# One-hots of two batches in one instruction, sums of sixteen tiles, and 48 columns of each column tile by VectorE, in a graph-attention kernel

## The chip, the core and the metric

The kernel runs on one core of a Trainium2 chip. The core has five engines with a queue each: TensorE (PE in the profile; its weight loads are listed apart as PEld), VectorE (DVE), ScalarE (ACT), GpSimd (POOL) and SyncE (SP), and 16 DMA engines that all of them share. An engine's sequencer takes the instructions of its queue in order; register loads, semaphore waits and the issuing of DMAs are done by the sequencer itself (DVEq, ACTq, SPq, POOLq in the profile) and do not count as busy time of the engine.

The metric is the device time of one execution in microseconds. It is measured over several runs, and the median is taken. Besides, one execution is recorded by the hardware profiler; its span runs from the first to the last instruction.

## What is computed

One layer of graph attention over 6250 nodes and 206250 edges, sorted by their destination `dst`, with 8 heads of 16 features. Cut to what matters, the reference is:

```
Qh = (x @ WQ).reshape(N, 8, 16);  Kh, Vh likewise with WK, WV
Eh = (edge_attr @ WE).reshape(E, 8, 16)
score = einsum('ehd,ehd,ehd->eh', Kh[src], Qh[dst], Eh) / sqrt(16)
score = exp(clip(score, -5, 5))
wV = segment_sum(Vh[src] * score[:, :, None], dst, N)
Z  = segment_sum(score, dst, N)
out = layernorm(x + (wV / (Z[:, :, None] + 1e-6)).reshape(N, 128))
```

## The kernel before

**Tiles and batches.** The edges are cut into 1612 tiles of 128. A batch (`cut_batches`) is four tiles; the last eight tiles make three batches of two and two of one, so there are 406 batches. In the head of the program a table `kv` of K and V rows of all nodes is made from `x` and written to HBM. Then one loop over the batches runs, written out in full. From batch 12 (`XB`) on, the order of the instructions on every engine is the order in which the program issues them (`tc.manual_schedule`); before that a planner of the framework orders them.

**One iteration b of the loop**, in the order in which it issues:

- Loads on SP: edge features (`load_chunk`, tiles of eight edge tiles in the pool `edges` with five buffers, two chunks ahead), the destination numbers relative to a window (`load_rel`), and Q rows (`load_q`).
- `stage_a(b)`, TensorE: `eps` (edge features times WE, L453) into the one PSUM buffer of `psE`, and `qps` (L456), which expands the Q rows to the edges by a one-hot `onehotT`.
- `gather` (L401), GpSimd: one indirect DMA for each edge tile fetches the 128 rows of `kv` into `kvrows`, twelve batches of buffers. A gather for batch b waits until TensorE has expanded batch b - `lag(b)`; the lag falls from 12 to 3 in the course of the run.
- `finish`, whenever two blocks of 128 nodes are complete: TensorE adds up the window sums that reach into the two blocks, each moved to its place by a shift matrix (`add_windows`, L492, into `finps`), ScalarE copies the result (`fin`), and a layernorm is put on a list. Its steps, some 22 small VectorE instructions beginning with `rz` (L727), are issued one at a time at the four `fill()` places of later iterations. The five steps that make 128 Q rows (`q_rows`, on VectorE `qst` and `qr`) go to the same places.
- VectorE, in this order: `kq` of batch b-1 (L463), one-hot of batch b+2 (`stage_0`, L431), fill, `kqe` of b-1 (L466), `onehotT` of b+2 (`stage_0t`, L441), fill, the reduce to `sc` of b-1 (L469), `msg` of b-2 (L507), column copies (L371), fill, the clip of `sc` (L472), fill. So in a batch each instruction of the chain kq, kqe, reduce has a one-hot of another batch between it and its successor.
- ScalarE: column copies (L374) in two portions, `place_columns` (L390), and `weigh` of b-1, which makes the weights that `msg` will need (L479, L480).
- `stage_c` of b-2, TensorE: the one-hot sums the messages of each tile into `agg` (L529). `project_columns`: a matmul makes K and V rows from a finished column tile (`colkv`, L383).

**Column tiles.** For 163 batches the fourth tile is not gathered. Its 128 columns of `x` are copied one by one from the transposed `x` in SBUF, to `xcol`, and projected by TensorE. The addresses are loaded into registers of the engine that copies, a run at a time: on ScalarE eleven runs of eight columns, one copy each; on VectorE five runs of eight columns, where one instruction takes two columns. `columns` issues as many runs as a due formula asks for up to this batch; `COLP`, `COLA` and `COLV` set the rate and the runs:

```
due = int((b - COL0 + COLL - 1 + share) * runs * COLP[1] / COLP[0] + 1e-6)
```

**One-hots and sums.** Eight consecutive tiles have their destinations inside a window of nodes. The first four tiles use a half of 64 nodes at its beginning, the other four one that begins 16 nodes later (`HALF`), and the two sets of buffers `halves` hold the one-hots of either kind, with the unused 64 columns set to zero once. `agg` holds two windows side by side; after 16 tiles ScalarE copies both to `sum` (L539).

**Edge numbers.** In the head, `from_window` reads the destinations of the edges (`dB_sb`), subtracts the first of each window (`relq`, L192) and stores them to HBM (`relD`, L193), from where `load_rel` reads them back. 128 rows come in the head, the other 74 at batch 14.

Of the kernel before, what the change touches and what calls it, by code (L numbers as in the profile page):

```python
# [20 lines left out]
B = 4  # L21
G = 4
HW = 64
HALF = 16
DRIFT = 24
MW = D + H
CH = 8
# [2 lines left out]
LOCK = XB + 6  # L30
STEP = 3
GLEAD = 2
OHB = (3, 5)
TAIL = 8
LAST = NT - TAIL
QL = N // P
# [11 lines left out]
QLOOK = 3  # L48
QREG = 16
COL0 = 24  # L50
COLP = (7, 3)
COLA = (8, 11)
COLV = (8, 5)
COLL = 8
RING = 4096
SUMS = 8
XT_AT = RING + P
NB = (N + P - 1) // P

# [16 lines left out]
    return [B * min(COL0 + k * COLP[0] // COLP[1], last - (n - 1 - k)) + B - 1 for k in range(n)]  # L76


def pair_of(t):

    return (t // (2 * G), t // G % 2) if t < LAST else (NT, 1)


def pair_start(k):

    return (2 * k * G * N + NT // 2) // NT - DRIFT


def window_start(t):
    k, half = pair_of(t)  # L90
    return QL * P + HW if k == NT else pair_start(k) + HALF * half


def q_built(j):
# [5 lines left out]
def edge_attention(ctx: ExitStack, tc: tile.TileContext, x, xT, srcT, srcC, dstT, dstB, dst0, bnd, lo, eaT,  # L100
# [24 lines left out]
    iota_f = cp.tile([P, P], F32, name="iota_f")  # L125
    shift = cp.tile([P, 3 * P], F32, name="shift")
    ident = cp.tile([P, P], F32, name="ident")
    halves = [[cp.tile([P, B, P], F32, name=f"onehot{h}{i}") for i in range(OHB[h])] for h in range(2)]
    cnt_i = cp.tile([1, 1], I32, name="cnt_i")

    batches = cut_batches()
# [8 lines left out]
    with ExitStack() as fast:  # L140
# [8 lines left out]
        nc.vector.tensor_scalar(shift[:HW], io_i[:HW], 0, None, op0=ALU.is_equal)  # L149
        nc.vector.tensor_scalar(shift[HW:], io_i[HW:], HALF - HW, None, op0=ALU.is_equal)  # L150
# [31 lines left out]
        def from_window(i):  # L182

            a, k = i * P, min(P, NJ - i * P)
            if i == len(dB_sb):
                dB_sb.append(ip.tile([P, WT * P], I32, name="dB_sb", bufs=1))
                nc.sync.dma_start(dB_sb[i][:k], dstB[a:a + k])
            d = dB_sb[i]
            w = ip.tile([P, 1], F32, name="wq0", bufs=2)
            nc.vector.tensor_tensor(w[:k], d[:k, :1], bnd_c[:k, i:i + 1], op=ALU.min)  # L190
            r = ip.tile([P, WT * P], BF16, name="relq", bufs=1)
            nc.vector.tensor_scalar(r[:k], d[:k], w[:k], None, op0=ALU.subtract)  # L192
            nc.sync.dma_start(relD[a:a + k], r[:k])  # L193
            cl = wp.tile([P, WT * P], F32, name="clq", tag="kvst", bufs=2)
            count(k, cl[:k], r[:k], QW - 1)
# [132 lines left out]
        def load_chunk(c):  # L328
            if c in chunks or c * CH >= NT:
                return  # L330
            n = min(CH, NT - c * CH) * P
            tl = ep.tile([P, CH * P], F32, name="ea")
            nc.sync.dma_start(tl[:, :n], eaT[:, c * CH * P:c * CH * P + n])
            chunks[c] = tl

# [8 lines left out]
            return max(STEP, 12 - (b - LOCK) // 40)  # L344

        col_tiles, xT_bytes = {}, spread.bitcast(U8)
        used = [0, 0]

        copied, projected = {}, []

        def columns(eng, b, share=1.0):

            size, runs = COLA if eng is nc.scalar else COLV
            first = 0 if eng is nc.scalar else COLA[0] * COLA[1]
            engine = mybir.EngineType.Activation if eng is nc.scalar else mybir.EngineType.DVE
            copy = eng.copy if eng is nc.scalar else eng.tensor_copy
            due = int((b - COL0 + COLL - 1 + share) * runs * COLP[1] / COLP[0] + 1e-6)
            while copied.get(engine, 0) < min(due, len(col_batches) * runs):
                k, j = divmod(copied.get(engine, 0), runs)
# [4 lines left out]
                at = nc.values_load_multi_w_load_instructions(  # L364
                    col_at[k % col_half:k % col_half + 1, k // col_half, j:j + size], engines=(engine,),
                    min_val=XT_AT, max_val=XT_AT + 8 * (N - 1) + 4,
                    skip_runtime_bounds_check_because="edges name nodes")[1]
                if eng is nc.vector:
                    for c in range(0, size, 2):
                        both = [xT_bytes[:, ds(a - XT_AT, 8)] for a in at[c:c + 2]]  # L370
                        eng.tensor_tensor(to[:, 4 * (j + c):4 * (j + c) + 8], *both, op=ALU.bitwise_or)  # L371
                    continue
                for c in range(size):
                    copy(to[:, 4 * (j + c):4 * (j + c) + 4], xT_bytes[:, ds(at[c] - XT_AT, 4)])  # L374
# [37 lines left out]
        def project(g, n):  # L412
# [6 lines left out]
            for i in range(0, n, 2):  # L419
# [3 lines left out]
                    nc.tensor.matmul(pk[:, j, :], xgT[:, i + j, :], wkv_sb, start=True, stop=True)  # L423
                nc.scalar.copy(g[:, i:i + k, :], pk[:, :k, :])

        def stage_0(b):
            t0, n = batches[b][0], len(batches[b])
            half = pair_of(t0)[1]
            oh = halves[half][used[half] % OHB[half]]
            used[half] += 1  # L430
            nc.vector.tensor_tensor(oh[:, :n, HW * half:HW * half + HW],  # L431
                                    iota_p[:, None, :].to_broadcast([P, n, HW]),
                                    rel[:, t0:t0 + n, None].to_broadcast([P, n, HW]), op=ALU.is_equal)
            st8[b] = oh, None

        def stage_0t(b):
            t0, n = batches[b][0], len(batches[b])
            oh = st8[b][0]
            ohT = wp.tile([QROWS, B * P], BF16, name="onehotT", bufs=AHEAD + 2)
            e0 = t0 % RC * P  # L440
            nc.vector.tensor_scalar(ohT[:, :n * P], rels[t0 // RC][:, e0:e0 + n * P], node[:QROWS], None,  # L441
                                    op0=ALU.is_equal)
            st8[b] = oh, ohT

        def stage_a(b, g):
            t0, n = batches[b][0], len(batches[b])
# [35 lines left out]

        def windows(q):

            return [(k, pair_start(k) - q * P) for k in range(min(NT, LAST + 2 * G - 1) // (2 * G))
                    if -HW - HALF < pair_start(k) - q * P < P]

        def add_windows(ps, q, first, stop):

            parts = windows(q)  # L490
            for i, (k, s) in enumerate(parts):
                nc.tensor.matmul(ps, shift[:, P - s:2 * P - s], sums[k // 2][:, k % 2],  # L492
                                 start=first and i == 0, stop=stop and i == len(parts) - 1)

        def finish(j):
# [16 lines left out]
        def stage_c(b):  # L512
            n, g, oh, m = st8.pop(b)
            for i in range(n):
                t = batches[b][i]
                k, half = pair_of(t)
# [5 lines left out]
                u = k if final else k // 2  # L522
                first = u not in aggs
                if first:
                    aggs[u] = psA.tile([P, 2, MW], F32, name="agg")
                    if final:
                        add_windows(aggs[u][:, 0], QL, True, False)
                tail = k == NT if t == NT - 1 else pair_of(t + 1)[0] != k
                nc.tensor.matmul(aggs[u][:, 0 if final else k % 2], oh[:, i, :], m[:, i, :],  # L529
                                 start=not final and t % (2 * G) == 0, stop=tail)  # L530
                if tail and final:
                    norms.extend(pending)
                    pending.clear()
                    while norms:
                        fill()
                    norms.append(layernorm(nc, sp, aggs.pop(u)[:, :1], xbs.pop(QL), out, QL, 1, stores))
                elif tail and (k % 2 == 1 or t == LAST - 1):
                    sums[u] = sp.tile([P, 2, MW], F32, name="sum", bufs=SUMS)
                    nc.scalar.copy(sums[u][:, :k % 2 + 1], aggs.pop(u)[:, :k % 2 + 1])  # L539
                    while len(finished) < QL // 2 and all(v // 2 <= u for v, _ in windows(2 * len(finished) + 1)):  # L540
                        ready.append(len(finished))
                        finished.append(u)

        gathered = {b: gather(b) for b in range(2)}
        for b0 in range(0, NB, KB):
# [251 lines left out]
```

## Time and profile before

| | us |
|---|---|
| median of 3 runs (lowest, highest) | 1867.37 (1865.28, 1867.83) |
| the profiled execution | 1864.63 |
| its span | 1862.8 |
| PE busy | 1331.3 |
| DVE busy | 1679.4 |
| ACT busy | 1623.1 |
| POOL busy | 1379.9 |

Rows of the profile are read as follows. A group: line, engine, operation, what it writes and reads, shapes, count, then busy time and the mean duration in ns, then the idle time just before the group's instructions and what ended most of it. A row of the waits: who waited for whom, the total in us, how often, the longest. A row of the timeline: start, duration, engine, line, operation; in square brackets idle time before it and its releaser, where "issue" is time in which the engine waited for nothing that the profile shows. A row of a table by stages: the stretch, its length, the busy time of the engine asked for with the number of instructions (x), the granted TensorE clock, the DMA share and GB/s. A row of one line: engine, operation, count, shortest, median and longest duration in ns, and the start of the first and the last in us. The mean granted TensorE clock of the profiled execution is 0.919.

### The profile page before, as it was taken

The numbers are of one execution on the slowest core, as the hardware profiler recorded it, in microseconds if no ns is written. First come the engines' busy times: TensorE is split into PE (matmuls) and PEld (weight loads), VectorE is DVE, ScalarE is ACT, GpSimd is POOL, SyncE is SP. The second block draws the span as 40 slices with busy tenths as digits, with TensorE's granted clock in tenths as the row PEclk, the third lists the DMA queues.
The fourth block names the chain that finished last, engine by engine and source line by source line (L and its number), as shares of the span: only waits on it lengthen the run. The fifth ranks groups of instructions, "written<-read, shape, count | busy, mean of one in ns | idle before, by whom it ended". The sixth has DMA issues, their size and how long they took to land.

```text
span 1862.8 us, 48831 instructions
## 1 busy us (share of the span) xinstructions
PE 1331.3 (71%) x9376; PEld 1163.7 (62%) x9376; DVE 1679.4 (90%) x6911; ACT 1623.1 (87%) x15506; POOL 1379.9 (74%) x1456
## 2 busy tenths in 40 slices
PE   4787777677776777676777776777767767677676
PEld 3576666666675666565666665666656656666665
DVE  3479999999999999999999999998999899998997
ACT  1236999899999999999999999999899999998993
POOL 6577777777777777777777777777777777777774
PEclk8898999899989998999999999898899899888998
DMA  9767757767777587677667667667766676667662
GB/s 316 220 196 213 219 179 209 207 201 207 207 215 208 180 241 199 184 217 228 192 209 228 190 191 225 203 185 214 219 203 186 195 231 191 195 192 227 207 195 70
DMA packets 171087, 381.63 MB, mean 205 GB/s; under 512 B 58478, under 2 KB 84412, under 8 KB 170774
## 3 DMA queue, kind: packets, MB, share of 16 engines
q0 software_dynamic: 68768, 186.80, 34.2%
q1 hardware_dynamic: 100866, 190.58, 33.7%
q14 instruction: 237, 1.94, 0.3%
q8 instruction: 76, 1.25, 0.3%
q10 hardware_dynamic: 1140, 1.06, 0.2%
HBM read 363.50 MB, written 14.81 MB: 203 GB/s over the span
## 4 chain that ended last, share of the span: by engine, by line
DVE 49%; PE 15%; DMA 12%; issue 6%; DVEq 6%; POOL 3%; ACT 0%; POOLq 0%
DMA kvrows<-kv,src 12%; DVE kqe L466 9%; DVE kq L463 9%; DVE xcol L371 8%; PE eps L453 6%; DVE sc L469 6%; DVE msg L507 5%; DVEq L364 5%; DVE onehot L431 5%; DVE onehotT L441 4%; PE agg L529 4%; POOL kvrows L401 3%; PE finps L492 3%; DVE sc L472 2%; PE qps L456 1%
## 5 line engine op out<-in xcount | busy, mean ns | idle before, releaser
L401 POOL DMA_INDIRECT kvrows<-kv,src x1401 | 1333.3, 952 | 441.9 <-issue 315.5
L374 ACT COPY xcol<-xT_sb 128x4 uint8 x14344 | 1442.7, 191 | 39.9 <-issue 33.9
L453 PE MATMUL eps<-we_sb,ea 128*128 128x128 f32 x3224 | 493.0, 300 | 446.5 <-issue 224.1
L453 PEld LDWEIGHTS eps<-we_sb,ea 128*128 128x128 f32 x3224 | 429.9, 206 | 538.6 <-issue 449.1
L529 PE MATMUL agg<-msg,onehot 128*128 128x136 f32 x3224 | 536.3, 314 | 34.0 <-DVE msg L507 23.2
L529 PEld LDWEIGHTS agg<-msg,onehot 128*128 128x128 f32 x3224 | 457.0, 212 | 86.1 <-DVE msg L507 83.5
L371 DVE TENSOR_TENSOR xcol<-xT_sb 128x8 uint8 x3260 | 301.8, 160 | 24.8 <-issue 22.2
L463 DVE TENSOR_TENSOR kq<-kvrows,qps 128x512 f32<-128x512 f32 x406 | 274.5, 676 | 51.0 <-DMA kvrows<-kv,src 26.7
L507 DVE TENSOR_TENSOR msg<-kvrows,exp_p 128x512 f32<-128x512 f32 x406 | 272.1, 670 | 4.0 <-ACT exp_p L480 4.0
L466 DVE TENSOR_TENSOR kqe<-kq,eps 128x512 f32<-128x512 f32 x406 | 272.9, 672 | 1.2 <-PE eps L453 0.8
L469 DVE TENSOR_REDUCE sc<-kqe 128x32 f32<-128x512 f32 x406 | 271.1, 668 | 0.2
L456 PE MATMUL qps<-qw,onehotT 126*128 126x128 bf16 x1612 | 169.6, 230 | 0.4 <-DVE kq L463 0.4
L431 DVE TENSOR_TENSOR onehot<-iota_p,dst_sb 128x256 f32<-128x256 f32 x406 | 167.4, 413 | 0.4 <-PE agg L529 0.4
L441 DVE TENSOR_SCALAR onehotT<-relb,node 126x512 bf16<-126x512 bf16 x406 | 148.3, 366 | 5.3 <-PE qps L456 2.7
L479 ACT ACTIVATE msg<-sc 128x32 f32<-128x32 f32 x406 | 92.9, 229 | 65.5 <-DVE sc L472 61.6
L456 PEld LDWEIGHTS <-onehotT 126*128 126x128 bf16 x1612 | 135.2, 104 | 9.4 <-issue 0.6
L383 PE MATMUL colkv<-wkv_sb,xcol 128*128 128x256 f32 x326 | 108.7, 418 | 0.0
L472 DVE TENSOR_SCALAR sc<-sc 128x32 f32<-128x32 f32 x406 | 84.5, 208 | 0.4
L492 PE MATMUL finps<-sum,shift 128*128 128x136 f32 x640 | 80.0, 282 | 0.0
L492 PEld LDWEIGHTS finps<-sum,shift 128*128 128x128 f32 x640 | 76.5, 191 | 0.0
L480 ACT ACTIVATE exp_p<-sc 128x32 f32<-128x32 f32 x406 | 74.1, 183 | 0.0
L401 POOL DMA_INDIRECT kvrows<-x,src x48 | 45.7, 952 | 21.2 <-issue 11.9
(73 smaller groups left out, 553.4 us busy)
## 6 DMA issues: line engine op xcount, KB each, us to landing
ea<-eaT SPq DMA_DIRECT2D x201, 512.0 KB
relb<-relD SPq DMA_DIRECT2D x100, 504.0 KB
kvrows<-kv,src POOLq DMA_INDIRECT x1401
qw<-qs SPq DMA_DIRECT2D x202, 31.5 KB
kv<-kvst SPq DMA_DIRECT2D x12, 512.0 KB
xT_sb<-xT SPq DMA_DIRECT2D x10, 521.0 KB
qs<-qst SPq DMA_DIRECT2D x48, 96.0 KB
xb<-x SPq DMA_DIRECT2D x24, 128.0 KB
```

The lines of the kernel that those rows point to most:

```text
L371: eng.tensor_tensor(to[:, 4 * (j + c):4 * (j + c) + 8], *both, op=ALU.bitwise_or)
L374: copy(to[:, 4 * (j + c):4 * (j + c) + 4], xT_bytes[:, ds(at[c] - XT_AT, 4)])
L401: ins = nc.gpsimd.indirect_dma_start(out=g[:k, i, :f], out_offset=None, in_=rows, in_offset=bass.IndirectOffsetOnAxis(ap=src_col(t)[:k], a ...
L431: nc.vector.tensor_tensor(oh[:, :n, HW * half:HW * half + HW], iota_p[:, None, :].to_broadcast([P, n, HW]), rel[:, t0:t0 + n, None].to_bro ...
L441: nc.vector.tensor_scalar(ohT[:, :n * P], rels[t0 // RC][:, e0:e0 + n * P], node[:QROWS], None, op0=ALU.is_equal)
L453: nc.tensor.matmul(pe[:, i, :], ea[:, i * P:i * P + P], we_sb, start=True, stop=True)
L456: expanded[b] = nc.tensor.matmul(pq[:, i, :], ohT[:, i * P:i * P + P], loaded[t0 // WT], start=True, stop=True)
L463: nc.vector.tensor_tensor(t0[:, :n], g[:, :n, :D], pq[:, :n], op=ALU.mult)
L466: nc.vector.tensor_tensor(t1[:, :n], t0[:, :n], pe[:, :n], op=ALU.mult)
L469: nc.vector.tensor_reduce(sc[:, :n], t1[:, :n].rearrange("p b (h d) -> p b h d", h=H), axis=AX.X, op=ALU.add)
L507: nc.vector.tensor_tensor(m[:, :n, :D].rearrange("p b (h d) -> p b h d", h=H), g[:, :n, D:].rearrange("p b (h d) -> p b h d", h=H), exp_p[ ...
L529: nc.tensor.matmul(aggs[u][:, 0 if final else k % 2], oh[:, i, :], m[:, i, :], start=not final and t % (2 * G) == 0, stop=tail)
```

## The change

The one-hots of two neighbouring batches are made by one instruction each (`onehot` and `onehotT`), where both batches have four tiles; the second of the two batches then issues none. The buffers are five tiles for two batches. A one-hot block keeps its 64 columns at a fixed place, with zeros around it, and a tile's offset in its window (0, 16, 32 or 48) is made by reading the block from so many columns earlier. Thus 16 tiles share one window of 128 nodes with one sum (`agg` and `sum` hold one window, not two), and `windows` lists fewer sums for each block of nodes. There are 167 column tiles, seven in 16 batches where there were three in seven; ScalarE copies ten runs of eight columns of each, VectorE six. The edge numbers go to a buffer of the pool `edges` and are loaded where `from_window` is called.

```diff
-HALF = 16
+QUAD = 4
+STEPS = 16
-OHB = (3, 5)
+OHB = 5
-COLP = (7, 3)
-COLA = (8, 11)
-COLV = (8, 5)
+COLP = (16, 7)
+COLA = (8, 10)
+COLV = (8, 6)
-SUMS = 8
+SUMS = 9
...
+def window_of(t):
+
+    return (t // (QUAD * G), STEPS * (t // G % QUAD)) if t < LAST else (NT, HW)
...
+def first_node(k):
+
+    return (QUAD * k * G * N + NT // 2) // NT - DRIFT
...
-    halves = [[cp.tile([P, B, P], F32, name=f"onehot{h}{i}") for i in range(OHB[h])] for h in range(2)]
+    onehots = [cp.tile([P, HW + 2 * B * P], F32, name=f"onehot{i}") for i in range(OHB)]
...
-        for h in range(2):
-            for tl in halves[h]:
-                nc.vector.memset(tl[:, :, HW - HW * h:P - HW * h], 0.0)
+        for tl in onehots:
+            nc.vector.memset(tl[:, :HW], 0.0)
+            nc.vector.memset(tl[:, HW:].rearrange("p (t n) -> p t n", n=P)[:, :, HW:], 0.0)
         nc.vector.tensor_copy(iota_f, io2)
-        dB_sb = [ip.tile([P, WT * P], I32, name="dB_sb", bufs=1)]
-        nc.scalar.dma_start(dB_sb[0][:min(P, NJ)], dstB[:min(P, NJ)])
...
-            if i == len(dB_sb):
-                dB_sb.append(ip.tile([P, WT * P], I32, name="dB_sb", bufs=1))
-                nc.sync.dma_start(dB_sb[i][:k], dstB[a:a + k])
-            d = dB_sb[i]
+            d = ep.tile([P, WT * P], I32, name="dB_sb", tag="ea")
+            (nc.sync if i else nc.scalar).dma_start(d[:k], dstB[a:a + k])
...
-                    col_tiles[k] = wp.tile([P, P], F32, name="xcol", bufs=4)
+                    col_tiles[k] = wp.tile([P, P], F32, name="xcol", bufs=5)
...
+        def together(b):
+
+            t0 = batches[b][0]
+            n = len(batches[b])
+            if n == B and b + 1 < nbat and len(batches[b + 1]) == B and t0 % (2 * B) == 0:
+                return [b, b + 1]
+            return [] if n == B and t0 % (2 * B) else [b]
+
         def stage_0(b):
...
+            group = together(b)
+            if not group:
+                return
+            t0, n = batches[b][0], sum(len(batches[i]) for i in group)
+            tl = onehots[used[0] % OHB]
+            used[0] += 1
+            nc.vector.tensor_tensor(tl[:, HW:].rearrange("p (t n) -> p t n", n=P)[:, :n, :HW],
                                     iota_p[:, None, :].to_broadcast([P, n, HW]),
                                     rel[:, t0:t0 + n, None].to_broadcast([P, n, HW]), op=ALU.is_equal)
-            st8[b] = oh, None
+            for i in group:
+                st8[i] = tl, HW + (batches[i][0] - t0) * P - window_of(batches[i][0])[1], None
 
         def stage_0t(b):
...
-            ohT = wp.tile([QROWS, B * P], BF16, name="onehotT", bufs=AHEAD + 2)
+            ohT = wp.tile([QROWS, 2 * B * P], BF16, name="onehotT", bufs=3)
...
-            return [(k, pair_start(k) - q * P) for k in range(min(NT, LAST + 2 * G - 1) // (2 * G))
-                    if -HW - HALF < pair_start(k) - q * P < P]
+            return [(k, first_node(k) - q * P) for k in range((LAST - 1) // (QUAD * G) + 1)
+                    if -HW - STEPS * (QUAD - 1) < first_node(k) - q * P < P]
...
-                nc.tensor.matmul(aggs[u][:, 0 if final else k % 2], oh[:, i, :], m[:, i, :],
-                                 start=not final and t % (2 * G) == 0, stop=tail)
+                nc.tensor.matmul(aggs[k][:, 0], oh[0][:, oh[1] + i * P:oh[1] + i * P + P], m[:, i, :],
+                                 start=not final and t % (QUAD * G) == 0, stop=tail)
...
-                elif tail and (k % 2 == 1 or t == LAST - 1):
-                    sums[u] = sp.tile([P, 2, MW], F32, name="sum", bufs=SUMS)
-                    nc.scalar.copy(sums[u][:, :k % 2 + 1], aggs.pop(u)[:, :k % 2 + 1])
+                elif tail:
+                    sums[k] = sp.tile([P, MW], F32, name="sum", bufs=SUMS)
+                    nc.scalar.copy(sums[k], aggs.pop(k)[:, 0])
```

More of the change, by code (lines that the diff above doesn't have):

```diff
@@ L76, in column_tiles @@
     return [B * min(COL0 + k * COLP[0] // COLP[1], last - (n - 1 - k)) + B - 1 for k in range(n)]
[L79 to L86, printed above, removed]
+def window_of(t):
+    return (t // (QUAD * G), STEPS * (t // G % QUAD)) if t < LAST else (NT, HW)
+def first_node(k):
+    return (QUAD * k * G * N + NT // 2) // NT - DRIFT
 def window_start(t):
-    k, half = pair_of(t)
-    return QL * P + HW if k == NT else pair_start(k) + HALF * half
+    k, at = window_of(t)
+    return (QL * P if k == NT else first_node(k)) + at
 def q_built(j):
@@ L331, in load_chunk @@
             n = min(CH, NT - c * CH) * P
-            tl = ep.tile([P, CH * P], F32, name="ea")
+            tl = ep.tile([P, CH * P], F32, name="ea", tag="ea")
             nc.sync.dma_start(tl[:, :n], eaT[:, c * CH * P:c * CH * P + n])
@@ L346, in edge_attention @@
         col_tiles, xT_bytes = {}, spread.bitcast(U8)
-        used = [0, 0]
+        used = [0]
         copied, projected = {}, []
@@ L424, in project @@
                 nc.scalar.copy(g[:, i:i + k, :], pk[:, :k, :])
-        def stage_0(b):
[L427 to L431, printed above, removed]
+        def together(b):
[4 more added lines that the diff above has]
+            return [] if n == B and t0 % (2 * B) else [b]
+        def stage_0(b):
+            group = together(b)
[5 more added lines that the diff above has]
+            nc.vector.tensor_tensor(tl[:, HW:].rearrange("p (t n) -> p t n", n=P)[:, :n, :HW],
                                     iota_p[:, None, :].to_broadcast([P, n, HW]),
                                     rel[:, t0:t0 + n, None].to_broadcast([P, n, HW]), op=ALU.is_equal)
-            st8[b] = oh, None
+            for i in group:
+                st8[i] = tl, HW + (batches[i][0] - t0) * P - window_of(batches[i][0])[1], None
         def stage_0t(b):
-            t0, n = batches[b][0], len(batches[b])
-            oh = st8[b][0]
-            ohT = wp.tile([QROWS, B * P], BF16, name="onehotT", bufs=AHEAD + 2)
+            group = together(b)
+            if not group:
+                return
+            t0, n = batches[b][0], sum(len(batches[i]) for i in group)
+            ohT = wp.tile([QROWS, 2 * B * P], BF16, name="onehotT", bufs=3)
             e0 = t0 % RC * P
@@ L442, in stage_0t @@
                                     op0=ALU.is_equal)
-            st8[b] = oh, ohT
+            for i in group:
+                tl, at, _ = st8[i]
+                k = (batches[i][0] - t0) * P
+                st8[i] = (tl, at), ohT[:, k:k + len(batches[i]) * P]
         def stage_a(b, g):
@@ L491, in add_windows @@
             for i, (k, s) in enumerate(parts):
-                nc.tensor.matmul(ps, shift[:, P - s:2 * P - s], sums[k // 2][:, k % 2],
+                nc.tensor.matmul(ps, shift[:, P - s:2 * P - s], sums[k],
                                  start=first and i == 0, stop=stop and i == len(parts) - 1)
@@ L515, in stage_c @@
                 t = batches[b][i]
-                k, half = pair_of(t)
+                k, _ = window_of(t)
                 q = t * N // NT // P
@@ L521, in stage_c @@
                 final = k == NT
[L522 to L525, printed above, removed]
+                if k not in aggs:
+                    aggs[k] = psA.tile([P, 1, MW], F32, name="agg")
                     if final:
-                        add_windows(aggs[u][:, 0], QL, True, False)
-                tail = k == NT if t == NT - 1 else pair_of(t + 1)[0] != k
-                nc.tensor.matmul(aggs[u][:, 0 if final else k % 2], oh[:, i, :], m[:, i, :],
-                                 start=not final and t % (2 * G) == 0, stop=tail)
+                        add_windows(aggs[k][:, 0], QL, True, False)
+                tail = t == NT - 1 or window_of(t + 1)[0] != k
+                nc.tensor.matmul(aggs[k][:, 0], oh[0][:, oh[1] + i * P:oh[1] + i * P + P], m[:, i, :],
+                                 start=not final and t % (QUAD * G) == 0, stop=tail)
                 if tail and final:
@@ L535, in stage_c @@
                         fill()
-                    norms.append(layernorm(nc, sp, aggs.pop(u)[:, :1], xbs.pop(QL), out, QL, 1, stores))
-                elif tail and (k % 2 == 1 or t == LAST - 1):
-                    sums[u] = sp.tile([P, 2, MW], F32, name="sum", bufs=SUMS)
-                    nc.scalar.copy(sums[u][:, :k % 2 + 1], aggs.pop(u)[:, :k % 2 + 1])
-                    while len(finished) < QL // 2 and all(v // 2 <= u for v, _ in windows(2 * len(finished) + 1)):
+                    norms.append(layernorm(nc, sp, aggs.pop(k), xbs.pop(QL), out, QL, 1, stores))
+                elif tail:
+                    sums[k] = sp.tile([P, MW], F32, name="sum", bufs=SUMS)
+                    nc.scalar.copy(sums[k], aggs.pop(k)[:, 0])
+                    while len(finished) < QL // 2 and all(v <= k for v, _ in windows(2 * len(finished) + 1)):
                         ready.append(len(finished))
-                        finished.append(u)
+                        finished.append(k)
         gathered = {b: gather(b) for b in range(2)}
```

3 lines of the change are left out of this document (1 added, 2 removed).

## The prediction

> **What bounds the kernel now.** I read the page's busy times first, then the gather line, then two tables of the same eight stages (GpSimd's gathers, VectorE's kq), then VectorE's waits, and last VectorE's timeline over three batches.
>
> ```profile
> PE 1331.3 (71%) x9376; PEld 1163.7 (62%) x9376; DVE 1679.4 (90%) x6911; ACT 1623.1 (87%) x15506; POOL 1379.9 (74%) x1456
> ...
> L401 POOL DMA_INDIRECT kvrows<-kv,src x1401: 904/946/1649, 81.7 to 1842.9; - x176
> ```
>
> The first line names VectorE and ScalarE, yet GpSimd, shown at 74%, is the engine without a gap: 1401 gathers start between 81.7 and 1842.9 us, one every 1.258 us (1761.2/1400). The 0.30 us between two of them is not counted as busy. It is a floor that only fewer gathers can lower. How near is VectorE to it? In the next fence the first two rows are gathers, the last five kq (one per batch of four tiles):
>
> ```profile
> 0.00:200.00 200.00, 134.08 (x140) 0.88 0.74 236
> 200.00:400.00 200.00, 151.49 (x160) 0.93 0.67 199
> ...
> 0.00:200.00 200.00, 19.09 (x28) 0.88 0.74 236
> 200.00:400.00 200.00, 30.06 (x45) 0.93 0.67 199
> 400.00:600.00 200.00, 31.82 (x47) 0.92 0.72 211
> 600.00:800.00 200.00, 31.22 (x46) 0.93 0.69 206
> 800.00:1000.00 200.00, 31.93 (x47) 0.96 0.70 207
> ```
>
> A batch needs 4 - 3/7 = 3.571 gathers; at 160 in 200 us that is 4.46 us a batch. VectorE did 185 batches in the 800 us from 200 to 1000: 4.32 us each. At 200 us it was some eight batches behind the gathers (140 gathers, 48 of them for the first twelve batches, the other 92 for about 24 more, against 28 kq), and it worked this off. Its waits, 200 to 1000 us in the first two rows, 1000 to 1800 in the third:
>
> ```profile
> DVE rz L727 <- ACT fin L502: 17.7, 11, 2.1
> DVE kq L463 <- DMA kvrows<-kv,src: 0.2, 1, 0.2
> ...
> DVE kq L463 <- DMA kvrows<-kv,src: 25.2, 15, 3.0
> ```
>
> Up to 1000 us VectorE practically never waits for a gather; it is saturated. After that it waits 25.2 us. So **two limits lie almost on each other**: GpSimd sets the end, and VectorE has about 26 us in the whole run to give away (0.07 us a batch). ScalarE is nearly as full, but the change takes work from it.
>
> **VectorE's batch.** Two neighbouring batches, the first with three runs of column copies, the second with two:
>
> ```profile
> 1434.81 0.69 DVE L463 TENSOR_TENSOR kq<-kvrows,qps 128x512 f32<-128x512 f32 x1 [0.24 <-PE qps L456]
> ...
> 1435.75 0.68 DVE L466 TENSOR_TENSOR kqe<-kq,eps 128x512 f32<-128x512 f32 x1
> ...
> 1437.80 0.70 DVE L371 TENSOR_TENSOR xcol<-xT_sb 128x8 uint8 x8
> 1438.82 0.40 DVE L371 TENSOR_TENSOR xcol<-xT_sb 128x8 uint8 x4 [0.32 <-issue]
> 1439.14 0.35 DVE L472 TENSOR_SCALAR sc<-sc 128x32 f32<-128x32 f32 x1
> 1439.22 0.68 DVE L463 TENSOR_TENSOR kq<-kvrows,qps 128x512 f32<-128x512 f32 x1
> 1439.82 0.41 DVE L431 TENSOR_TENSOR onehot<-iota_p,dst_sb 128x256 f32<-128x256 f32 x1
> 1440.15 0.67 DVE L466 TENSOR_TENSOR kqe<-kq,eps 128x512 f32<-128x512 f32 x1
> 1440.75 0.34 DVE L441 TENSOR_SCALAR onehotT<-relb,node 126x512 bf16<-126x512 bf16 x1
> 1441.01 0.67 DVE L469 TENSOR_REDUCE sc<-kqe 128x32 f32<-128x512 f32 x1
> ...
> 1442.87 0.37 DVE L472 TENSOR_SCALAR sc<-sc 128x32 f32<-128x32 f32 x1
> 1442.95 0.68 DVE L463 TENSOR_TENSOR kq<-kvrows,qps 128x512 f32<-128x512 f32 x1
> ```
>
> Starts matter, not durations: an independent instruction begins some 0.07 us before its forerunner ends. From kq to kq the two-run batch takes 3.73 us, the three-run batch 4.41: 0.68 more, though four copies take only 0.32 (1438.82 to 1439.14). The rest is the 0.32 us idle with "issue" before the third run. What is late there is the load of that run's addresses:
>
> ```profile
> L364 DVEq TENSOR_LOAD <-col_at x815: 591/606/1001, 152.5 to 1822.7; - x163
> ...
> 547.09 0.68 DVE L466 TENSOR_TENSOR kqe<-kq,eps 128x512 f32<-128x512 f32 x1
> ...
> 549.46 1.09 DVE L371 TENSOR_TENSOR xcol<-xT_sb 128x8 uint8 x12
> 550.47 0.42 DVE L729 TENSOR_TENSOR h<-fin,rz 128x256 f32<-128x256 f32 x1
> ```
>
> Every run needs one such load of 0.606 us by VectorE's sequencer, and three in a batch come one after the other. The other three-run batch shown, in which a layernorm step and a slow onehotT lay in the way, has no idle before its third run, and still takes 3.38 us from kqe to the end of its copies (547.09 to 550.47), like the first with 3.39 (1435.75 to 1439.14). So **in a three-run batch the sequencer sets 3.39 us behind kqe, whatever VectorE does meanwhile**.
>
> [...]
>
> **The change, part by part (VectorE).** Columns: 163 tiles x 5 runs = 815 become 167 x 6 = 1002. By the due formula in `columns`, batches with three runs go from 54 to 238, with two from 326 to 144. The one-hots of two batches now fall into every even iteration (143 with three runs, 48 with two), odd iterations have none (95 and 96).
>
> A one-hot of 512 elements appears nowhere; kqe has that size and also reads the matmul banks: 0.60 us from start to start, against 2 x 0.33. onehotT of 1024 isn't shown either:
>
> ```profile
> L441 DVE TENSOR_SCALAR onehotT<-relb,node 126x512 bf16<-126x512 bf16 x401 | 146.7, 366 | 5.3 <-PE qps L456 2.7 <-DMA relb<-relD 2.5
> ...
> L441 DVE TENSOR_SCALAR onehotT<-relb,node 126x128 bf16<-126x128 bf16 x2 | 0.5, 250 | 0.0
> ...
> 78.51 0.68 DVE L469 TENSOR_REDUCE sc<-kqe 128x32 f32<-128x512 f32 x1
> 79.22 0.18 DVE L472 TENSOR_SCALAR sc<-sc 128x32 f32<-128x32 f32 x1
> ```
>
> Rows 128 and 512 give 116 ns for 384 elements, so 512 more cost 0.155 us; nothing saved at all would be 0.26. I take 0.15 on top of today's 0.26. [...] In odd iterations kqe follows kq, and the reduce follows kqe, with nothing between. A dependent pair is shown by the last two rows: 79.22 - 78.51 = 0.71, against 0.60, so 0.11 lost twice.
>
> Per batch then:
> - even, three runs: 0.60 + 0.60 + 3.39 + 0.08 (sc to kq) = 4.67
> - even, two runs: 0.60 + 0.60 + 2.72 (1440.15 to 1442.87) + 0.15 + 0.08 = 4.15
> - odd, three runs: 0.71 + 3.39 + 0.08 = 4.18
> - odd, two runs: 0.71 + 2.72 - 0.26 + 0.11 + 0.08 = 3.36
>
> 143 x 4.67 + 48 x 4.15 + 95 x 4.18 + 96 x 3.36 = 1587 us, against 54 x 4.41 + 326 x 3.73 and two lone ones of 3.4 = 1461: **+126 us**. Without any saving from the doubled onehotT it would be 5 us more, since the loads cover it in the three-run batches.
>
> Given back, first: q-row and layernorm steps (some 720, four places a batch, so one in 0.47 of the batches at each place). One behind onehotT costs about 0.2 us in a two-run batch and nothing in a three-run one: 184 more of those x 0.47 x 0.2 = 17 us. In odd batches such a step also fills the dependent gaps: 0.47 x 0.11 x (191 + 96) = 15 us. Together **-32** (bounds 0 and -40).
>
> Second, `finish`, of which there are 24: the shifted sums of `windows` drop from 320 to 185 matmuls, or 640 records to 370, 11 fewer per finish.
>
> ```profile
> 300.00:600.00 300.00, 13.39 (x108) 12.79 (x108) 1.54 (x4) 0.91 0.69 203
> ...
> DVE rz L727 <- ACT fin L502: 36.4, 22, 3.3
> ```
>
> The first row is the finps tile: 0.124 us a record, so 1.4 us earlier. The second is the wait behind it, 1.65 us each: it nearly vanishes, **-30** (bounds -20 and -36). Shorter ScalarE work (984 column copies fewer, narrower sum copies) may bring message weights earlier: 0 to -15, I take **-3**.
>
> VectorE: 126 - 32 - 30 - 3 = +61 us.
>
> **Other engines.** GpSimd: 4 gathers fewer, -5.0 us of its floor, which no longer sets the end. ScalarE loses 984 of 14344 copies:
>
> ```profile
> L374 ACT COPY xcol<-xT_sb 128x4 uint8 x14344 | 1442.7, 191 | 39.9 <-issue 33.9
> ...
> 12.29 0.16 DVE L190 TENSOR_TENSOR wq<-dB_sb,bnd_c 128x1 f32<-128x1 int32 x1 [3.06 <-DMA bnd_c<-bnd]
> 12.48 0.81 DVE L192 TENSOR_SCALAR relq<-dB_sb,wq 128x1024 bf16<-128x1024 int32 x1
> ...
> 28.99 0.50 SPq L193 DMA_DIRECT2D relD<-relq  x1
> ```
>
> 1442.7/14344 = 0.10 each: -99 us, plus the sums; nothing waits for it long, so worth nothing itself. TensorE's saved 33 us (270 x 0.124) lie beside VectorE's work except at finish. The edge-number load moves behind the tables on ScalarE's queue; relq ends at 13.3 but its store leaves SP at 28.99, so 15.7 us cover the delay; without cover all would start later by it (0 to 5). On SP the second piece takes an edge buffer at batch 14, behind which edges, q windows and rel loads queue; two chunks are loaded ahead, so nothing. The larger memsets (about 1 us more) come before an idle stretch of 3.06 us on VectorE. The last finish saves 1.4 us in the tail.
>
> **The sum.** Span 1862.8 + 61 - 26 (VectorE's spare waits) - 1.4 = 1896.4. The profiled execution took 1864.63, 1.8 more than its span; the median of the runs is 2.7 above that. So 1896.4 + 1.8 + 2.7 = **1901 us**.
>
> **Rivals.** **A, the loads hide and GpSimd still ends it (the other side).** If the sequencer ran ahead, three-run batches would cost 0.32 less: even 4.67 - 0.32 + 0.15 = 4.50, odd 4.18 - 0.32 - 0.15 = 3.71, in all 143 x 4.50 + 48 x 4.15 + 95 x 3.71 + 96 x 3.36 = 1518, or +57; minus 15, 30 and 3 leaves +9, inside the 26 us. Then the end follows the gathers: -5.0 - 1.4, or 1861. It decides as soon as VectorE's growth stays below about 20 us. For it: today's two-run batches, 326 of 380, show no such idle. Against it: both three-run batches shown.
>
> **B, TensorE is late for the short odd batches.**
>
> ```profile
> L453 PE MATMUL eps<-we_sb,ea 128*128 128x128 f32 x3224 | 493.0, 300 | 446.5 <-issue 224.1
> ...
> L456 PE MATMUL qps<-qw,onehotT 126*128 126x128 bf16 x1612 | 169.6, 230 | 0.4 <-DVE kq L463 0.4
> ```
>
> eps needs its bank back, so it starts when kqe is done, 0.67 after kqe's start. It takes 1.22 us a batch (493.0 over 403 batches of eight records), qps 0.42: ready 2.31 after kqe's start, and the short batch asks for it at 2.65. Whatever else holds TensorE for over 0.34 us there makes kq wait; at 0.3 in each of the 96 batches that is +29, and with ten of the finish's thirty microseconds not coming back, +39: 1940. For it: the margin is small. Against: no wait of kq for qps is among the large ones above.
>
> **C, what is given back is larger** (steps and ScalarE at their bounds, 26 us): 1875, still slower.
>
> **Chances.** Forecast 0.57 (1880 to 1922), C 0.14, A 0.16, B 0.13. A change within 0.2%, 3.7 us, can't be told from none by this measurement. Faster 0.14 (most of A), same 0.05, slower 0.81. Range: 1863 to 1936; the forecast's own is 1880 to 1922.
>
> **What would show it.** Right: GpSimd's gathers spread out (gaps over 0.30 us that end with qps, the pace they are held to), kq hardly waiting for gathers after 1000 us, the "issue" idle before column copies up from 22 to over 50 us, kqe to sc at 3.39 us in three-run batches, rz's wait below 10 us, kq counts near 44.5 per 200 us from the start. Wrong: gathers still 1.25 us apart up to the end, or a third run without idle before it.

## The result, and the profile after

| | before | after |
|---|---|---|
| median of 5 runs (lowest, highest), us | 1867.65 (1865.28, 1869.42) | 1918.14 (1908.72, 1920.95) |
| span of the profiled execution, us | 1862.8 | 1906.9 |

The change makes the kernel slower: the ratio is 1.0264, with a 95% interval of 1.0245 to 1.0283, or 50 us. The profiled execution of the changed kernel is the quickest of its five runs.

The line numbers are those of the changed kernel. Its busy times and its gather line:

```profile
PE 1317.5 (69%) x9112; PEld 1164.1 (61%) x9112; DVE 1729.4 (91%) x7260; ACT 1557.7 (82%) x14526; POOL 1379.2 (72%) x1452
...
L397 POOL DMA_INDIRECT kvrows<-kv,src x1397: 902/946/1557, 78.3 to 1887.4; - x200
```

TensorE and ScalarE have less to do, GpSimd the same, VectorE 50 us more. The gathers begin earlier than before (78.3 against 81.7 us), but 1396 intervals now fill 1809.1 us, 1.296 us each where it was 1.258. What stopped them is in GpSimd's waits, the row of before first and then that of the changed kernel:

```profile
POOL kvrows L401 <- PE qps L456: 11.3, 37, 0.3
...
POOL kvrows L397 <- PE qps L468: 43.7, 38, 3.0
```

Before, these were 37 waits of at most 0.3 us, which is the ordinary gap between two gathers put down to whatever ended last. Now there are waits of up to 3.0 us. They end with `qps`, and a gather is held to the qps matmul of an earlier batch. GpSimd has become the engine that waits. VectorE's own waits, two rows of before first:

```profile
DVE kq L463 <- DMA kvrows<-kv,src: 26.7, 18, 3.0
DVE xcol L371 <- issue: 22.2, 71, 0.6
...
DVE xcol L367 <- issue: 64.7, 184, 0.8
...
DVE rz L737 <- ACT fin L514: 11.8, 13, 2.4
...
DVE wq L186 <- DMA dB_sb<-dstB: 4.7, 1, 4.7
...
DVE kq L475 <- DMA kvrows<-kv,src: 1.2, 4, 0.4
```

kq waited 26.7 us for gathers before, and now 1.2: VectorE's spare time is used up. The wait for `fin` has shrunk from 36.4 us to 11.8, and the idle time ahead of column copies has grown from 22.2 us to 64.7. VectorE's pace, as kq in 200 us:

```profile
0.00:200.00 200.00, 18.40 (x27) 0.86 0.75 236
200.00:400.00 200.00, 29.20 (x43) 0.90 0.66 196
400.00:600.00 200.00, 29.89 (x44) 0.90 0.66 194
600.00:800.00 200.00, 30.02 (x45) 0.89 0.70 208
800.00:1000.00 200.00, 30.36 (x45) 0.88 0.67 196
```

177 batches from 200 to 1000 us are 4.52 us each, 0.20 more than before, and longer than the 4.46 of the gathers. VectorE falls further behind instead of catching up. Four batches of VectorE's timeline, one of each kind that the prediction priced:

```profile
606.25 0.69 DVE L475 TENSOR_TENSOR kq<-kvrows,qps 128x512 f32<-128x512 f32 x1
606.85 0.68 DVE L437 TENSOR_TENSOR onehot<-iota_p,dst_sb 128x512 f32<-128x512 f32 x1
607.45 0.68 DVE L478 TENSOR_TENSOR kqe<-kq,eps 128x512 f32<-128x512 f32 x1
608.05 0.48 DVE L450 TENSOR_SCALAR onehotT<-relb,node 126x1024 bf16<-126x1024 bf16 x1
608.44 0.68 DVE L481 TENSOR_REDUCE sc<-kqe 128x32 f32<-128x512 f32 x1
...
610.52 0.40 DVE L367 TENSOR_TENSOR xcol<-xT_sb 128x8 uint8 x4 [0.19 <-issue]
610.83 0.38 DVE L484 TENSOR_SCALAR sc<-sc 128x32 f32<-128x32 f32 x1
610.92 0.68 DVE L475 TENSOR_TENSOR kq<-kvrows,qps 128x512 f32<-128x512 f32 x1
611.63 0.69 DVE L478 TENSOR_TENSOR kqe<-kq,eps 128x512 f32<-128x512 f32 x1
612.36 0.69 DVE L481 TENSOR_REDUCE sc<-kqe 128x32 f32<-128x512 f32 x1
...
614.73 0.40 DVE L367 TENSOR_TENSOR xcol<-xT_sb 128x8 uint8 x4 [0.37 <-issue]
615.05 0.18 DVE L484 TENSOR_SCALAR sc<-sc 128x32 f32<-128x32 f32 x1
615.13 0.68 DVE L475 TENSOR_TENSOR kq<-kvrows,qps 128x512 f32<-128x512 f32 x1
...
619.29 0.68 DVE L475 TENSOR_TENSOR kq<-kvrows,qps 128x512 f32<-128x512 f32 x1
...
628.27 0.68 DVE L475 TENSOR_TENSOR kq<-kvrows,qps 128x512 f32<-128x512 f32 x1
...
631.65 0.68 DVE L475 TENSOR_TENSOR kq<-kvrows,qps 128x512 f32<-128x512 f32 x1
```

From kq to kq, the even batch with three runs takes 4.67 us (606.25 to 610.92), the odd one 4.21 (610.92 to 615.13), the even batch with two runs 4.16 (615.13 to 619.29), the odd one 3.38 (628.27 to 631.65). In both three-run batches the last four copies are announced by idle time with "issue": they wait for their addresses. The profile has the loads of these addresses too, three for each of these two batches:

```profile
L360 DVEq TENSOR_LOAD <-col_at x3: 599/600/602, 608.2 to 609.8; - x3
...
L360 DVEq TENSOR_LOAD <-col_at x3: 598/603/619, 612.4 to 614.0; - x3
```

In both batches the first load starts when kqe has just ended (607.45 + 0.68 = 608.13 and 611.63 + 0.69 = 612.32), and the third starts 1.6 us later, so it ends at 610.4 and 614.6. The last four copies start 0.1 us after that.

### The profile page after: what moved, and what is told of

It is laid out like the page before. It is cut to its first block, busy times and chain, and to the rows that moved or that the text cites. A ratio compares the mean times of both kernels' runs of the same rounds, so it can differ in the third digit from the quotient of the medians.

```text
span 1906.9 us, 47742 instructions
## 1 busy us (share of the span) xinstructions
PE 1317.5 (69%) x9112; PEld 1164.1 (61%) x9112; DVE 1729.4 (91%) x7260; ACT 1557.7 (82%) x14526; POOL 1379.2 (72%) x1452
## 4 chain that ended last, share of the span: by engine, by line
DVE 53%; DMA 13%; PE 12%; issue 9%; POOL 6%; DVEq 6%; ACT 2%; ACTq 0%; POOLq 0%; SPq 0%
DMA kvrows<-kv,src 10%; DVE xcol L367 10%; DVE kqe L478 9%; DVE kq L475 9%; DVE sc L481 6%; POOL kvrows L397 6%; DVE msg L519 6%; DVEq L360 5%; PE eps L465 4%; DVE onehot L437 4%; DVE onehotT L450 3%; PE agg L539 2%; DVE sc L484 2%; PE finps L504 2%; DMA kv<-kvst 2%
## 5 line engine op out<-in xcount | busy, mean ns | idle before, releaser
L370 ACT COPY xcol<-xT_sb 128x4 uint8 x13360 | 1363.2, 190 | 93.8 <-issue 84.0
L465 PE MATMUL eps<-we_sb,ea 128*128 128x128 f32 x3224 | 505.5, 305 | 497.1 <-issue 317.3
L465 PEld LDWEIGHTS eps<-we_sb,ea 128*128 128x128 f32 x3224 | 438.1, 210 | 595.1 <-issue 529.7
L539 PE MATMUL agg<-msg,onehot 128*128 128x136 f32 x3224 | 552.7, 321 | 40.0 <-DVE msg L519 38.9
L539 PEld LDWEIGHTS agg<-msg,onehot 128*128 128x128 f32 x3224 | 474.0, 219 | 72.6 <-DVE msg L519 65.0
L367 DVE TENSOR_TENSOR xcol<-xT_sb 128x8 uint8 x4008 | 376.2, 160 | 69.2 <-issue 64.7
L475 DVE TENSOR_TENSOR kq<-kvrows,qps 128x512 f32<-128x512 f32 x406 | 274.0, 675 | 20.2 <-PE qps L468 12.8
L437 DVE TENSOR_TENSOR onehot<-iota_p,dst_sb 128x512 f32<-128x512 f32 (+2 forms) x206 | 137.8, 670 | 2.0 <-PE agg L539 2.0
L450 DVE TENSOR_SCALAR onehotT<-relb,node 126x1024 bf16<-126x1024 bf16 (+2 forms) x206 | 102.1, 496 | 1.6 <-DMA relb<-relD 1.6
L379 PEld LDWEIGHTS colkv<-wkv_sb,xcol 128*128 128x128 f32 x334 | 60.0, 220 | 2.1 <-ACT xcol L370 2.1
L386 ACT COPY kvrows<-colkv 128x256 f32<-128x256 f32 x167 | 60.3, 361 | 0.8 <-PE colkv L379 0.8
```

Of the source, the lines that this page charges most:

```text
L379: nc.tensor.matmul(pk, col_tiles.pop(k), wkv_sb, start=True, stop=True)
L437: nc.vector.tensor_tensor(tl[:, HW:].rearrange("p (t n) -> p t n", n=P)[:, :n, :HW], iota_p[:, None, :].to_broadcast([P, n, HW]), rel[:, t ...
L465: nc.tensor.matmul(pe[:, i, :], ea[:, i * P:i * P + P], we_sb, start=True, stop=True)
L475: nc.vector.tensor_tensor(t0[:, :n], g[:, :n, :D], pq[:, :n], op=ALU.mult)
L539: nc.tensor.matmul(aggs[k][:, 0], oh[0][:, oh[1] + i * P:oh[1] + i * P + P], m[:, i, :], start=not final and t % (QUAD * G) == 0, stop=tail)
```

## The experiments

Theory 1 was that the loss lies in VectorE's column runs, above all in the third address load of a batch. Theory 2 put it on the pairing, theory 3 on the head and the edge buffer. Each ratio below is to the kernel before, run beside it on the same chip (medians 1863.71 us with the first four, 1864.14 with the others). With the result above it was 1867.65 us, so kernels of different groups are compared by what each is above or below its own before.

| kernel | median us | ratio (95% interval) |
|---|---|---|
| column shares of before | 1867.06 | 1.0016 (1.0006 to 1.0025) |
| before, with the column edits alone | 1959.91 | 1.0518 (1.0498 to 1.0539) |
| VectorE's runs split in two | 1867.45 | 1.0012 (1.0003 to 1.0022) |
| one address load for each batch | 1866.70 | 1.0020 (1.0009 to 1.0031) |
| one-hots of one batch | 1910.92 | 1.0255 (1.0238 to 1.0273) |
| split, one-hots of one batch | 1860.13 | 0.9983 (0.9974 to 0.9993) |
| the same, edge numbers in their own buffer | 1857.06 | 0.9958 (0.9944 to 0.9972) |
| the same, second piece loaded at batch 8 | 1862.51 | 0.9988 (0.9978 to 0.9997) |

### The column shares of before

```diff
-COLP = (16, 7)
-COLA = (8, 10)
-COLV = (8, 6)
+COLP = (7, 3)
+COLA = (8, 11)
+COLV = (8, 5)
```

> The changed kernel with the column shares of before: 163 column tiles, eleven runs by ScalarE and five by VectorE; the paired one-hots, the sums of sixteen tiles and the edge buffer stay. Theory 1 (the cost lies in VectorE's column runs, above all in the third address load of a batch): VectorE falls back below the gathers' pace, the gathers are 1.25 us apart again, and the time is 1860 to 1870. Theory 2 (the cost lies in the pairing: dependent instructions with nothing between them in odd batches, and bursts in even ones): 1895 or more, VectorE still over 4.45 us a batch. Theory 3 (the head or the edge buffer start everything later): the first kv gather or the first kq late by 5 us or more, the time 1870 to 1880.

1867.06 us, 3.4 us above before: 47 of the 50 us of the loss are gone with three numbers. Pairing, sums and edge buffer together leave 3 us. Theories 2 and 3 fall as the main cause.

### The column edits alone

The same three lines the other way round in the kernel before, with five column buffers.

> The kernel before with nothing but the column edits: 167 column tiles, ten runs by ScalarE and six by VectorE, five column buffers. Theory 1: all of the loss and more, since the shorter finish is missing: 54 three-run batches become 238 (+126 us), about 17 given back by hidden steps, 26 by spare waits: 1930 to 1955, rz waiting for fin 25 us or more. Theory 2 (pairing): within 15 us of before, 1860 to 1882.

1959.91 us, 96 us above before and 5 above the range that theory 1 gave. So the other edits of the change are a gain of some 46 us (96 less 50) once VectorE is the limit. The wait for `fin` is larger than it was before the change, 45.0 us against 36.4:

```profile
DVE xcol L371 <- issue: 65.5, 202, 0.7
DVE rz L727 <- ACT fin L502: 45.0, 24, 3.8
```

### One address load for each batch

```diff
+            at = None
             while copied.get(engine, 0) < min(due, len(col_batches) * runs):
...
+                if at is None or eng is nc.scalar:
                     at = nc.values_load_multi_w_load_instructions(
```

> The changed kernel with one address load for each batch on VectorE: the second and third run of a batch copy from the addresses of the first, so the K and V rows of the column tiles are not those of the reference. The number of copies is the same, 601 or more of the 1002 loads are gone. Theory 1 with the sequencer: no idle before the third run, kqe to the clip of sc about 3.0 us instead of 3.39 in three-run batches, the gathers set the end: 1858 to 1870. If the copies cost: above 1900.

1866.70 us, with all 4008 column copies still there; of the 1002 loads 382 are left. The row of copies that wait with "issue" is gone from VectorE's waits, and a three-run batch shows its twelve copies in one piece:

```profile
517.93 0.68 DVE L477 TENSOR_TENSOR kq<-kvrows,qps 128x512 f32<-128x512 f32 x1
518.64 0.69 DVE L480 TENSOR_TENSOR kqe<-kq,eps 128x512 f32<-128x512 f32 x1
519.37 0.69 DVE L483 TENSOR_REDUCE sc<-kqe 128x32 f32<-128x512 f32 x1
519.97 0.68 DVE L521 TENSOR_TENSOR msg<-kvrows,exp_p 128x512 f32<-128x512 f32 x1
520.57 1.04 DVE L369 TENSOR_TENSOR xcol<-xT_sb 128x8 uint8 x12
521.53 0.17 DVE L486 TENSOR_SCALAR sc<-sc 128x32 f32<-128x32 f32 x1
521.62 0.68 DVE L477 TENSOR_TENSOR kq<-kvrows,qps 128x512 f32<-128x512 f32 x1
```

This is an odd batch. From kqe to the clip of `sc` 2.89 us pass, where the odd batch of the changed kernel took 3.42, and from kq to kq 3.69 instead of 4.21: the same twelve copies, with nothing idle ahead of them. Since the copies are all there, and all but 3.0 of the 50 us went with 620 loads, **not the copies but the loads of their addresses**, which the sequencer takes one after the other (0.83 us apart on the median in the changed kernel), made the columns dear.

### VectorE's runs split in two

```diff
                 stage_0(b + AHEAD)
+            if b < nbat:
+                columns(nc.vector, b, 0.5)
             fill()
```

> The changed kernel with VectorE's column runs of a batch in two portions: half of what is due after the one-hot, ahead of kqe, the rest where all were. The work is the same. Theory 1 with the sequencer as its cause: the first load runs beside kq and the one-hot, no third load waits behind kqe, and the copies fill the gap between kq and kqe in odd batches; by the rows 143 x 0.23 + 95 x 0.45 = 76 us less on VectorE, so the gathers set the end: 1858 to 1872, idle with issue before the copies below 30 us. If it is the number of copies, not the loads, that costs: above 1900.

1867.45 us, 3.7 above before: the same work in another place costs 47 us less. In the program the loads and copies of the first portion now stand between kq and kqe. The idle time with "issue" is below what it was before the change, and gathers are waited for again:

```profile
DVE xcol L367 <- issue: 18.1, 46, 0.8
DVE kq L475 <- DMA kvrows<-kv,src: 14.6, 17, 3.7
```

### One-hots of one batch

```diff
-            if n == B and b + 1 < nbat and len(batches[b + 1]) == B and t0 % (2 * B) == 0:
-                return [b, b + 1]
-            return [] if n == B and t0 % (2 * B) else [b]
+            return [b]
```

Buffers for the one-hots go with it: eight of four tiles, and four for onehotT.

> The changed kernel with one-hots of one batch each (eight buffers of four tiles, four onehotT buffers); columns, sums of sixteen tiles and the edge buffer as changed. Theory 1: pairing is nearly neutral where three runs lie in a batch, since the loads set 3.39 us behind kqe either way: 238 x 4.41 + 144 x 3.73 = 1587 us, the same sum as with pairs, and about 15 us less is given back: 1910 to 1935, and 25 to 45 us faster than the kernel with the column edits alone, by the shorter finish. Theory 2 (pairing is the cost): 1890 or less.

1910.92 us, at the low end of the range. Its interval overlaps that of the changed kernel (1.0245 to 1.0283): with three runs in most batches it makes no difference that can be told whether the one-hots are paired. Against the column edits alone it is 49 us faster, more than the 25 to 45 expected from the shorter finish. This kernel's wait of `rz` is 7.3 us against 45.0, which is 38 of the 49; the rest isn't traced.

### Towards a version that beats both

> The split of VectorE's runs, with one-hots of one batch each. VectorE stays below the gathers' pace (238 x 4.04 + 144 x 3.73 = 1499 us, finish 30 shorter), so only GpSimd is asked. If the longer onehotT of the pairs holds up the gathers (18.7 us of gather time over 946 ns each with the split and pairs, 9.1 before), this kernel is back near 9 to 11 us and at 1856 to 1865. If it doesn't matter, the same as the split with pairs, 1864 to 1870.

> As the split with one-hots of one batch, and the edge numbers in a buffer of their own again, loaded where the kernel before loads them. If the edge buffer makes the second piece late, the wait for it falls from about 5 us to 3.5 and the gap in the gathers near 145 us from 4.9 to about 2.8: 2 us less than with the edge buffer. If not: equal.

> As the one with the edge numbers in a buffer of their own, but the second piece is loaded at batch 8 instead of 14. If VectorE's wait for it is what stops the gathers near 145 us, that gap goes (below 1 us) and the time falls by 2 to 4 us against the one that loads it at batch 14: 1853 to 1862. If something else is late there, the gap stays.

The edits are those of the two sections above together, then the lines for `dB_sb` of the kernel before, then that load at batch 8. The first gave 1860.13 us, within the range; but the gathers' time over 946 ns each (added up over those that took longer) is 13.2 us, between the two figures that the expectation set against each other. With the own buffer it is 7.8 us and the time 1857.06, **0.42% below the kernel before and the fastest of all**. The wait for the second piece fell from 4.9 us to 3.6 and the gap near 145 us from 4.5 to 3.3: that is 1.3 us where 2 were expected, and of the 3 us between the two medians the rest isn't explained.

The two gather lines, of the split with pairs first, of the fastest kernel second:

```profile
L397 POOL DMA_INDIRECT kvrows<-kv,src x1397 | 1339.8, 959 | 444.9 <-issue 323.7 <-DVE msg L519 21.8 <-DVE kq L475 12.8
...
L401 POOL DMA_INDIRECT kvrows<-kv,src x1397 | 1328.1, 951 | 444.2 <-issue 312.8 <-DVE msg L521 21.7 <-PE eps L467 11.9
```

The difference is 11.7 us of gather time, while the idle time before the gathers is the same: the gathers set the end in both. Each row is of one execution, the slowest of its kernel (1874.3 and 1860.7 us), so the 11.7 us explain the 13.6 between these two and not exactly the 10 between the medians. The traces show where they come from. Half of the gathers took at least 949 ns in the first and 946 in the second; the 48 gathers in the head show the same 3 ns (947 and 944). Two kernels with single one-hots have them as well and three with pairs don't, so these 4 us in 1397 gathers don't come from pairing. Nearly all of the rest lies in gathers during which VectorE was making an `onehotT`: with pairs 230 gathers, on the mean 48 ns over the 949; with single one-hots 404, 10 ns over the 946. All others are 3 ns over in both. The other kernels agree: these gathers are 28 to 48 ns over in the four with pairs, 5 to 12 in the six with single ones. So **the gathers that met the longer onehotT took longer**; why, no row tells. In all they lose 6 to 11 us in an execution with pairs, and 2 to 5 with single ones.

Loading the second piece at batch 8 removed VectorE's wait for it and the gap in the gathers near 145 us, as expected. But the time is 1862.51, above the expected range. In the profiled execution the first gather from `kv` started at 87.4 us instead of 80.9. The early load goes out on SP at 63.4 us, ahead of the store of Q rows (`qs`) that the first kq needs; that store took 11.1 us to land where it took 5.5 without the early load, and kq's longest wait for `qps` was 13.8 us instead of 7.7, in one execution of each. What was gained at batch 14 was less than what was lost in the head.

## Why the prediction was right

**The two limits.** The prediction had GpSimd at its floor and VectorE with 26 us to spare. All of the spare time went (kq's wait for gathers 26.7 to 1.2 us), and the end then followed VectorE. Where VectorE was relieved, in three experiments, the time came back to the gathers' pace.

**The price of a batch.** Predicted 4.67, 4.15, 4.18 and 3.36 us, measured in the rows above 4.67, 4.16, 4.21 and 3.38. The step on which it rests, that the sequencer sets 3.39 us from kqe to the end of a third run whatever VectorE does, shows as 3.38 (607.45 to 610.83) and 3.42 (611.63 to 615.05), though one batch has an onehotT of 1024 in the way and the other nothing. The rows of the loads show what the first load of a batch waited for. In 373 of the 382 batches with loads the first one starts within 0.1 us of the end of kqe, and in 229 of the 382 before the reduce, which needs kqe's result, has itself begun. So the sequencer came to the loads when kqe had ended, 0.05 us after it on the median, and not when VectorE had come to the instructions ahead of them: in all 382 batches `msg` had yet to begin. Each further load of a batch starts 0.83 us after the one before, on the median. From kqe's start that makes 0.68 + 0.05 + 2 x 0.83 + 0.60 = 3.0 us to the end of the third load, and with 0.1 to the first of its copies and 0.3 for the four of them 3.4. Whether the reduce itself holds the sequencer or `msg` behind it can't be told, since both stand between kqe and the load. In the split kernel, with loads placed ahead of kqe, 47 of the 50 us are gone.

**The rows that before did not have.** The one-hot of 512 elements takes 0.60 us to the next start, as kqe did. onehotT of 1024 takes 0.39 (608.05 to 608.44), so 512 elements more cost 0.13. The 0.15 from the two rows was a little high, which moves the total by 1 us. A dependent pair costs 0.11 over the 0.60 (kq to kqe 0.71) and 0.13 (kqe to reduce 0.73).

**What was mis-sized.** The loss was to be 34 us and is 50; the span was to be 1896.4 and is 1906.9, the median 1901 and is 1918. The terms that failed are those of what VectorE is given back. By the two tables VectorE lost 0.20 us a batch (4.32 to 4.52), some 76 us in 382 batches, where the sum had 126 - 65 = 61. Of the 15 us between, the finish accounts for 5: it gave back 24.6 us of waiting (36.4 to 11.8) instead of 30, and so missed the sign of less than 10. The other 10 lie in the hidden steps and the earlier weights, which no row shows apart. Against this the loop began 3.4 us earlier, which the sum didn't have. That gives 1862.8 + 76 - 26 - 1.4 - 3.4 = 1908, near the measured span. The remaining 7 us of the median come from the profiled execution: it was taken to be 2.7 us below the median and was 9.4 below, the quickest of the five.

**The rivals.** C went the other way, less was given back and not more; its 26 us need the finish at its bound too, since the steps and ScalarE alone make 20. B, TensorE late for the short odd batches, didn't come: kq waited 12.8 us for qps, 14.7 before. A had the later part right: with the loads out of the way GpSimd ends it. But A put such a kernel 6 us below before, and the two kernels that are like it are 3.0 and 3.7 above (one load for each batch, and the split). Four gathers fewer saved nothing there, because each gather took longer: 956 and 959 ns on the mean, against 952 before. The prediction took the gathers' pace as a floor that the one-hots can't change, and gave this no term.

**The head.** The edge numbers' later load cost nothing at the start, as predicted (the first kq is at 73.4 us, before at 76.8); at batch 14 VectorE waited 4.7 us for the second piece instead of 3.5, where the forecast had nothing.

## What to carry to other kernels

In the kernel before, VectorE was busy for 90% of the span and GpSimd, at 74%, set the end: look for gaps between the instructions that repeat without end (0.30 us between gathers here), and for how much the nearest rival waits on them. Work added to VectorE was free here up to this wait of some 26 us and cost time beyond it. Before giving an engine more small instructions that take addresses from registers, price the loads on its sequencer (0.606 us each here) and ask which instruction ahead of them has to wait: the loads behind such a wait came late here, and with the first portion of the same loads a few lines earlier the kernel was 3.7 us above before instead of 50. Before making two instructions into one, ask whether they are on the path. Here another chain set the batch and they saved nothing that can be told (ratio 1.0264 with pairs, 1.0255 without), and the gathers that met the longer instruction took 28 to 48 ns over the median, against 5 to 12.

## What the runs showed of the hardware that was not expected

A register load of VectorE's sequencer took longer with more addresses, but not in proportion: 606 ns for eight, and 311 ns for the one address that is loaded once, at L637 of the kernel before. On SyncE the first row below has thirteen loads, twelve of sixteen addresses and a last one of ten, which at 1150 ns is hardly shorter:

```profile
L311 SPq TENSOR_LOAD <-starts x13: 1150/1165/1254, 69.5 to 1721.5; - x13
...
L637 DVEq TENSOR_LOAD <-cnt_i x1: 311/311/311, 433.3 to 433.3; - x1
L637 SPq TENSOR_LOAD <-cnt_i x1: 452/452/452, 434.0 to 434.0; - x1
```

Whether fewer and larger loads on VectorE would have been cheaper no run shows. And GpSimd's gathers, with the same work to do, took from 951 to 959 ns on the mean in the profiled executions, up to 11 us in a run. Part of that is a difference of 3 ns that is already there in the head, part the gathers that meet a paired onehotT. With two limits this close, 11 us is twice as much as the four gathers saved by the change.
